# A graph layer on one core: a new order of the sums, scans, powers and table terms over the five steps of a turn

## The chip, the core and the metric

The kernel runs on one core of a Trainium2 chip. The metric is the device time of one execution in microseconds. Before the change the median of three runs is 2198.17 us (2196.62 to 2205.42). The core has five engines that run side by side, each strictly in the order of its own queue: PE (TensorE, matrix products), DVE (VectorE), ACT (ScalarE), POOL (GpSimd, here the issuer of the gathers) and SP (the issuer of nearly all other transfers).

## What is computed

The layer has 12,500 nodes of 128 features and 212,500 edges, sorted by the node they point to (dst). Cut to what matters:

```python
h  = maximum(layernorm(x), 0)
q  = h @ Wq.T + bq;  v = h @ Wv.T + bv          # per node, 8 heads of 16
k  = edge_attr @ Wk.T + bk                      # per edge
in_m   = sum(q[src] * k,      over the 16 of a head)
out_m  = sum(q[dst] * k,      over the 16 of a head)
diag_m = sum(q[src] * q[dst], over the 16 of a head)
score = (segment_softmax(in_m / 4, dst) + segment_softmax(out_m / 4, dst)
         + segment_softmax(diag_m / 4, dst)) * edge_weight ** lam
out = segment_sum(score * v[dst], dst) @ Wo.T + bo
return x + leaky_relu(out, 0.1)
```

## The kernel before

**Staging.** A first part (some 130 us) normalizes the nodes, makes q and writes it to a table in memory, turns the edge indices, and writes a second table, `q3_table`, that holds q as three bf16 terms whose sum is q. The borders of the edges' segments are made behind the table of q. Then comes the main loop of 415 steps: step g takes a block of 512 edges. Five steps s = 0 to 4 make a turn t; the five blocks of a turn come from five far-apart parts of the sorted edge list, so that five parts are scanned side by side (120 rows: 5 parts x 24 logits). There are 83 turns. A short tail closes the last turns and the last nodes.

**One step.** POOL fetches q[src] of the 512 edges by four indirect gathers (tile `qq`, line 694), started up to 20 steps ahead (`LOOK`); a gather of step g + 20 may start when PE is through with step g. PE projects the edge features to k (L1165 the bias, L1167 the products) and spreads q[dst] over the edges by a one-hot product (L1175), both into one of two buffers of `kq_ps`; it also transposes the features of the step after (L1158). PE makes the k of step g + 1 in step g, so it has to wait until DVE's products of step g - 1 have freed the buffer. ACT copies q[dst] out (`qd`, L1178), copies the transposed features (`eT`, L1160) and makes one-hots (L1152, L1153). DVE multiplies (`prod`, L1188 and L1189), and a sum over the heads makes the logits (L1194, `lT`). Two steps share one `prod` tile: the sum runs over a pair of steps, or over the one step left over, as five is odd.

**One turn.** Spread over the steps, each turn also has:

- `turn_logits`: PE transposes the turn's logits to rows (`l_ps`, L1215); `scan_on`: DVE scans them forward for the running maximum of each segment (`u`, L1248, and a short `head`, L1253). This is done for turn t - 1.
- `spread_far` (ACT, L1259), then `scan_back`: DVE scans backward (`m`, L1266); `turn_max`: PE transposes the maxima back (`m_ps`, L1336). This and the rest is for turn t - 2.
- `powers`: DVE subtracts the maxima (`back`, L1344), ACT takes the exponentials (L1345); `weigh_powers`: DVE multiplies by the edge weights (L1356).
- `show_ends`: PE makes selection matrices (`d_ps`, L1370), ACT shapes them (`sel`, L1373 twice, L1374); `to_rows`: PE sums by node (`w_ps`, L1384), ACT copies (L1389), SP adds the rows to memory (L1400).
- `other_terms`: for 40 of the turns, the three bf16 terms of the next 256 nodes' q: SP loads them, ACT rounds (L1288), DVE subtracts (L1289), ACT rounds again (L1291), DVE subtracts (L1292), SP writes (L665).
- Nodes: 20 pairs of 256 nodes each are finished within the loop, each over four turns: `scores` (L1034 to L1040), `turn` (PE L1084, ACT `hT` L1087), `project_v` (PE L1090, L1092) and `weigh` (DVE L1100) in the first two turns; `turn`, `project_o` (PE, then ACT L1111) and `add_x` (DVE L1116, L1117) in the next.

**What sets the order.** The order is written out by hand: `pin` ties every instruction behind the one recorded before it on its engine. Within a step the main loop calls, in this order, `nodes_before`, the gather, `project`, `spread_q`, `turn`, `logits`, `one_hots`, then the piece of the turn for this s, the fetches and stores of rows, `nodes_between` and (for s below 3) `other_terms`. All small PSUM results (`l_ps`, `far_ps`, `m_ps`, `d_ps`, `w_ps`, `node_ps`) share three buffers in rotation, so each one waits for the release of the third before it.

## Time and profile before

| | us |
|---|---|
| median of three runs | 2198.17 |
| the profiled execution | 2201.97 |
| its span (first to last instruction) | 2200.1 |
| DVE busy | 1961.2 (89% of the span) |
| PE busy | 1715.9 (78%) |
| POOL busy | 1595.9 (73%) |
| ACT busy | 1414.0 (64%) |
| mean granted TensorE clock | 0.795 of full |

In a row of a timeline the first number is the start in us from the span's start, the second the length in us; then engine, line, operation and tiles, and in brackets how long the engine sat idle before it and what ended the wait. In a list of waits, the three numbers are us in total, times, and the longest. In a table of stretches each engine's busy us stand with the number of its instructions, then the granted clock.

### The profile page before, as it was taken

The page shows a single profiled execution, that of the slowest core. Times are in us where ns is not written, and L with a number is a line of the kernel's source. Part 1 is how long each engine was busy: PE and PEld are TensorE (multiplying, and loading weights), DVE is VectorE, ACT ScalarE, POOL GpSimd, SP SyncE. Part 2 cuts the span into 40 slices and gives each one's busy share as a digit, 9 for nine tenths or more (in the row PEclk, how much of TensorE's full clock was granted, in tenths as well). Part 3 has the DMA queues.
Part 4 walks back from the last instruction along what each step waited for, and adds up shares of the span by engine and source line. Part 5 has one row for each costly group of instructions (what it writes and reads, how often), then busy time and mean ns, then how long its engine had stood idle before and what let it go on. Part 6 is the DMA issues. An engine that isn't in the chain of part 4 may idle for free.

```text
span 2200.1 us, 34526 instructions
## 1 busy us (share of the span) xinstructions
PE 1715.9 (78%) x10337; PEld 1370.5 (62%) x10337; DVE 1961.2 (89%) x2144; ACT 1414.0 (64%) x2639; POOL 1595.9 (73%) x1678
## 2 busy tenths in 40 slices
PE   7767787787878788887788778777777888877886
PEld 5556566565666666666666666666565666666665
DVE  7759999999898989899998999998999899888985
ACT  8846666566665666666666666666666666666681
POOL 5677777777777777777777777777777777777740
PEclk9868888888787877788877777887888777877787
DMA  9695545545554555555554655555555554555522
GB/s 266 177 260 148 179 146 175 156 149 181 152 156 148 181 161 158 154 156 184 157 153 152 192 159 147 158 177 154 157 158 185 153 154 145 155 162 152 161 85 64
DMA packets 306063, 355.66 MB, mean 162 GB/s; under 512 B 118195, under 2 KB 225661, under 8 KB 305557
## 3 DMA queue, kind: packets, MB, share of 16 engines
q1 hardware_dynamic: 237094, 238.23, 35.0%
q0 software_dynamic: 53184, 108.92, 17.6%
q10 hardware_dynamic: 15588, 6.22, 1.1%
q8 instruction: 83, 1.36, 0.2%
q14 instruction: 114, 0.93, 0.1%
HBM read 321.34 MB, written 31.85 MB: 161 GB/s over the span
## 4 chain that ended last, share of the span: by engine, by line
PE 37%; DVE 28%; DMA 12%; issue 10%; ACT 5%; POOL 3%; SPq 1%; DVEq 0%; ACTq 0%; POOLq 0%
PE kq_ps L1167 13%; DMA qq<-q_table,src_i 12%; DVE prod L1189 9%; DVE lT L1194 8%; PE w_ps L1384 6%; PE eT_ps L1158 5%; DVE prod L1188 5%; PE kq_ps L1165 3%; DVE u L1248 3%; PE kq_ps L1175 3%; POOL qq L694 3%; PE node_ps L1092 3%; PE d_ps L1370 2%; PE l_ps L1215 1%; ACT eT L1160 1%
## 5 line engine op out<-in xcount | busy, mean ns | idle before, releaser
L694 POOL DMA_INDIRECT qq<-q_table,src_i x1620 | 1544.5, 953 | 493.7 <-issue 232.5
L1167 PEld LDWEIGHTS kq_ps<-wk,eT 128*128 128x128 f32 x3320 | 524.5, 241 | 371.0 <-issue 154.4
L1194 DVE TENSOR_REDUCE lT<-prod 128x192 f32<-128x3072 f32 (+1 forms) x249 | 702.1, 2820 | 8.6
L1167 PE MATMUL kq_ps<-wk,eT 128*128 128x128 f32 x3320 | 619.8, 344 | 8.6 <-ACT eT L1160 8.2
L1178 ACT COPY qd<-kq_ps 128x512 f32<-128x512 f32 x415 | 242.3, 584 | 426.2 <-PE kq_ps L1175 396.1
L1189 DVE TENSOR_TENSOR prod<-qq,kq_ps 128x1024 f32<-128x1024 f32 x415 | 503.4, 1213 | 0.0
L1165 PE MATMUL kq_ps<-b,ones 3*128 3x512 bf16 x415 | 184.6, 445 | 217.8 <-DVE prod L1189 217.8
L1158 PE MATMUL eT_ps<-ident,ea 128*128 128x128 f32 x1660 | 324.4, 331 | 1.0 <-DVE qq L944 1.0
L1152 ACT ACTIVATE relb<-relb,before 114x512 bf16<-114x512 bf16 x415 | 302.6, 729 | 0.0
L1188 DVE TENSOR_TENSOR prod<-qd,kq_ps 128x512 f32<-128x512 f32 x415 | 279.8, 674 | 12.5 <-ACT qd L1178 7.7
L1153 ACT ACTIVATE oh<-relb 114x512 bf16<-114x512 bf16 x415 | 261.4, 630 | 13.6 <-ACT relb L1152 0.4
L1160 ACT COPY eT<-eT_ps 128x512 f32<-128x512 f32 x415 | 244.0, 588 | 36.6 <-PE eT_ps L1158 36.0
L1384 PE MATMUL w_ps<-back,sel 128*114 128x144 f32 (+1 forms) x1344 | 215.5, 322 | 20.5 <-DVE back L1356 11.7
L1158 PEld LDWEIGHTS eT_ps<-ident,ea 128*128 128x128 f32 x1660 | 229.8, 175 | 1.1 <-DVE qq L944 1.1
L1384 PEld LDWEIGHTS w_ps<-back,sel 128*114 128x114 f32 (+1 forms) x1344 | 207.8, 213 | 27.0 <-ACT sel L1374 10.1
L1336 PE MATMUL m_ps<-ident,m 120*128 120x120 f32 x332 | 69.8, 342 | 176.0 <-DVE m L1266 176.0
L1175 PE MATMUL kq_ps<-win,oh 114*128 114x128 bf16 x1660 | 199.9, 255 | 2.7 <-DMA win<-q_table 2.7
L1248 DVE TENSOR_TENSOR_SCAN u<-far,u,l_ps 120x512 f32<-120x512 bf16 x82 | 104.7, 1277 | 94.2 <-PE l_ps L1215 88.2
L1345 ACT ACTIVATE back<-back 128x480 f32<-128x480 f32 x83 | 50.1, 604 | 202.9 <-DVE back L1344 202.9
L1336 PEld LDWEIGHTS m_ps<-ident,m 120*128 120x128 f32 x332 | 49.7, 214 | 198.5 <-DVE m L1266 195.7
L1175 PEld LDWEIGHTS <-oh 114*128 114x128 bf16 x1660 | 161.2, 118 | 15.6 <-issue 2.9
L1266 DVE TENSOR_TENSOR_SCAN m<-far_ps,head,u 120x512 f32<-120x512 f32 x81 | 103.2, 1274 | 0.0
(194 smaller groups left out, 1481.2 us busy)
## 6 DMA issues: line engine op xcount, KB each, us to landing
ea<-in_edge_attr_dram SPq DMA_DIRECT2D x83, 1280.0 KB
relb<-rel_d SPq DMA_DIRECT2D x83, 640.0 KB
qq<-q_table,src_i POOLq DMA_INDIRECT x1620
win<-q_table SPq DMA_DIRECT2D x415, 28.5 KB
far<-far_d SPq DMA_DIRECT2D x84, 120.2 KB
q_table<-more_q SPq DMA_DIRECT2D x40, 192.0 KB
sums<-rows SPq DMA_DIRECT2D x408, 7.1 KB
q_table<-xq SPq DMA_DIRECT2D x24, 256.0 KB
```

The lines of the kernel that those rows point to most:

```text
L694: rows = pin(nc.gpsimd.indirect_dma_start(out=qq[:, j, :], out_offset=None, in_=x if g < RAW else q_table, in_offset=bass.IndirectOffsetOn ...
L1152: pin(nc.scalar.activation(d, d, AF.Abs, bias=before[:K3]))
L1153: pin(nc.scalar.activation(oh, d, AF.Relu, bias=1.0, scale=-1.0))
L1158: pin(nc.tensor.transpose(eT_ps[:, j, :], eas[g // S][:, g % S, j * F:(j + 1) * F], ident))
L1160: pin(nc.scalar.copy(eT, eT_ps))
L1165: pin(nc.tensor.matmul(k_ps, ones3, bk3, start=True, stop=False))
L1167: pin(nc.tensor.matmul(k_ps[:, j, :], eTs[g][:, j, :], wk, start=False, stop=(j == JN - 1)))
L1175: pin(nc.tensor.matmul(qd_ps[:, j, :], ohs[g][:, j * P:(j + 1) * P], d["win"][:, s, :], start=(j == 0), stop=(j == JN - 1)))
L1188: pin(nc.vector.tensor_mul(prod[:, :, 2, :], qds[g], kqs[g][:, 0]))
L1189: pin(nc.vector.tensor_mul(prod[:, :, 0:2, :], qqs[g][:, :, None, :].to_broadcast([P, JN, 2, F]), kqs[g].rearrange("p i j f -> p j i f")))
L1194: pin(nc.vector.tensor_reduce(lTs[t][:, :, lo:s + 1, :].rearrange("p j s c -> p j (s c)"), prods[0][:, :, :s + 1 - lo].rearrange("p j s i ...
L1384: pin(nc.tensor.matmul(w_ps[:, i].rearrange("p s c -> p (s c)"), d["sel"][:n, j, lo:lo + 3, :].rearrange("p s w -> p (s w)"), d["back"][:n ...
```

## The change

The same work is done; only its place in the turn differs.

- The pairs of the sum are cut otherwise: step 0 alone, then steps 1 and 2, then 3 and 4 (before: 0 and 1, 2 and 3, then 4 alone).
- `scan_on` moves from step 0 to step 1, right ahead of `scan_back`.
- `powers` moves from step 2 to step 3, behind `show_ends`; `weigh_powers` stays in step 3 but goes to the end of the step, behind the nodes' work and `other_terms`.
- `other_terms` is spread over steps 1, 3, 4 and the next turn's step 0, begins one turn earlier, and has two buffers for each of its tiles.
- Nodes: `project_o` moves from step 4 to step 2, `add_x` from 4 to 3, `scores` from 0 to 3.

```diff
-            if s % 2 == 0:
+            lo = max(0, s - 1 + s % 2)
+            if s == lo:
                 prods[0] = work.tile([P, JN, 2, 3, F], F32, name="prod", bufs=1)
-            prod = prods[0][:, :, s % 2]
+            prod = prods[0][:, :, s - lo]
...
-            if s % 2 == 1 or s == S - 1:
-                lo = s - s % 2
+            if s % 2 == 0:
                 pin(nc.vector.tensor_reduce(
...
         def other_terms(t, s):
 
-            if s == 0 and other_units and due_at[other_units[0]] <= t + 5:
-                held["u"] = other_units.pop(0)
-            if not held:
-                return
-            u = held["u"]
-            if s == 0:
-                held["q"] = work.tile([P, 2, F], F32, name="more_q", bufs=1)
+            if s == 0 and "u" in held:
+                q3 = held["q3"]
+                pin(nc.vector.tensor_sub(q3[:, :, 2, :], held["q"], q3[:, :, 1, :]))
+                put_terms(held["u"], q3)
+                held.clear()
+            if s == 0 and other_units and due_at[other_units[0]] <= t + 6:
+                u = held["u"] = other_units.pop(0)
+                held["q"] = work.tile([P, 2, F], F32, name="more_q", bufs=2)
                 pin(nc.sync.dma_start(held["q"].rearrange("p k f -> p (k f)"),
                                       units(q_table, u, 1, F)[:, 0, :]))
-            elif s == 2:
-                q3 = held["q3"] = work.tile([P, 2, 3, F], BF, name="more_q3", bufs=1)
-                pin(nc.scalar.copy(q3[:, :, 0, :], held["q"]))
-                pin(nc.vector.tensor_sub(held["q"], held["q"], q3[:, :, 0, :]))
+            if "u" not in held:
+                return
+            if s == 1:
+                held["q3"] = work.tile([P, 2, 3, F], BF, name="more_q3", bufs=2)
+                pin(nc.scalar.copy(held["q3"][:, :, 0, :], held["q"]))
             elif s == 3:
+                pin(nc.vector.tensor_sub(held["q"], held["q"], held["q3"][:, :, 0, :]))
+            elif s == 4:
                 pin(nc.scalar.copy(held["q3"][:, :, 1, :], held["q"]))
-                pin(nc.vector.tensor_sub(held["q3"][:, :, 2, :], held["q"], held["q3"][:, :, 1, :]))
-                put_terms(u, held["q3"])
-                held.clear()
...
-            if old and t % 2 == 0 and s == 4:
+            if old and t % 2 == 0 and s == 2:
                 old.project_o(small([P, JN, F], "node_ps"))
...
-            if new and not even and s == 0:
+            if new and not even and s == 3:
                 new.scores()
...
-            if old and even and s == 4:
+            if old and even and s == 3:
                 old.add_x(nc.vector)
...
             if s == 0:
                 if t > 0:
                     turn_logits(t - 1)
-                    scan_on(t - 1)
...
             elif s == 1:
+                later(scan_on, t - 1)
                 later(scan_back, t - 2)
...
             elif s == 2:
                 later(turn_max, t - 2)
-                later(powers, t - 2)
                 fetch_places(t + 2)
             elif s == 3:
                 later(show_ends, t - 2)
-                later(weigh_powers, t - 2)
-                other_terms(t, s)
+                later(powers, t - 2)
                 fetch(t + 2)
...
-            if s < 3:
-                other_terms(t, s)
+            other_terms(t, s)
+            if s == 3:
+                later(weigh_powers, t - 2)
```

The two product lines become 1189 and 1190, and the lines behind `other_terms` move down by one (L1344 becomes L1345). On DVE, the queue around the two scans. Before (u is the forward scan, m the backward one, lT the sums, ab and score the nodes' scores):

```order
L1188 TENSOR_TENSOR prod<-qd,kq_ps 128x4x128
L1189 TENSOR_TENSOR prod<-qq,kq_ps 128x4x256
L1248 SCALAR_TENSOR_TENSOR u<-far,u,l_ps 120x512
L1253 SCALAR_TENSOR_TENSOR head<-far,u 120x64
L1034 TENSOR_TENSOR ab<-ab 128x4x48
...
L1040 TENSOR_TENSOR score<-score,ab 128x32
L1188 TENSOR_TENSOR prod<-qd,kq_ps 128x4x128
L1189 TENSOR_TENSOR prod<-qq,kq_ps 128x4x256
L1194 TENSOR_REDUCE lT<-prod 128x4x48
L1266 SCALAR_TENSOR_TENSOR m<-far_ps,head,u 120x512
```

and with the change, from step 0 on:

```order
L1189 TENSOR_TENSOR prod<-qd,kq_ps 128x4x128
L1190 TENSOR_TENSOR prod<-qq,kq_ps 128x4x256
L1194 TENSOR_REDUCE lT<-prod 128x4x24
L1189 TENSOR_TENSOR prod<-qd,kq_ps 128x4x128
L1190 TENSOR_TENSOR prod<-qq,kq_ps 128x4x256
L1248 SCALAR_TENSOR_TENSOR u<-far,u,l_ps 120x512
L1253 SCALAR_TENSOR_TENSOR head<-far,u 120x64
L1266 SCALAR_TENSOR_TENSOR m<-far_ps,head,u 120x512
```

The forward scan now stands a whole step behind the products of step 0, and the backward one directly behind it, ahead of the pair's sum instead of behind it.

On DVE again, the powers, in a turn with a unit of `other_terms` (and, in the second, with an `add_x`). Before:

```order
L1344 TENSOR_TENSOR back<-lT,m_ps 128x20x24
L1289 TENSOR_TENSOR more_q<-more_q,more_q_11655 128x256
L1188 TENSOR_TENSOR prod<-qd,kq_ps 128x4x128
L1189 TENSOR_TENSOR prod<-qq,kq_ps 128x4x256
L1194 TENSOR_REDUCE lT<-prod 128x4x48
L1356 TENSOR_TENSOR back<-back,att_t 128x20x24
```

With the change:

```order
L1194 TENSOR_REDUCE lT<-prod 128x4x48
L1189 TENSOR_TENSOR prod<-qd,kq_ps 128x4x128
L1190 TENSOR_TENSOR prod<-qq,kq_ps 128x4x256
L1345 TENSOR_TENSOR back<-lT,m_ps 128x20x24
L1116 TENSOR_TENSOR h<-h,node_ps 128x512
L1117 TENSOR_TENSOR x_in<-h,x_in 128x512
L1293 TENSOR_TENSOR more_q<-more_q,more_q_11359 128x256
L1357 TENSOR_TENSOR back<-back,att_t 128x20x24
```

A step's products and a pair's sum stood between the subtraction and the weighing; now only nodes' work and a subtraction of `other_terms` stand there, in the turns that have them.

On ACT, the exponentials of the same step (`sel` is the selection matrix, `back` the powers). Before:

```order
L1345 ACTIVATE back<-back 128x20x24
L1288 CAST more_q_12139<-more_q 128x2x128
L1178 COPY qd<-kq_ps 128x512
L1160 COPY eT<-eT_ps 128x512
L1152 ACTIVATE relb<-relb,before 114x512
L1153 ACTIVATE oh<-relb 114x512
L1373 ACTIVATE sel<-d_ps 128x380 x2
L1374 ACTIVATE sel<-sel 128x760
```

With the change:

```order
L1178 COPY qd<-kq_ps 128x512
L1160 COPY eT<-eT_ps 128x512
L1152 ACTIVATE relb<-relb,before 114x512
L1153 ACTIVATE oh<-relb 114x512
L1374 ACTIVATE sel<-d_ps 128x380 x2
L1375 ACTIVATE sel<-sel 128x760
L1346 ACTIVATE back<-back 128x20x24
```

The exponentials stood ahead of the four regular instructions of a step and the three of `sel`; now they stand behind them.

## The prediction

> **What bounds the kernel now.** I read the page's busy times first, then how fast each engine moves through the main loop.
>
> ```profile
> PE 1715.9 (78%) x10337; PEld 1370.5 (62%) x10337; DVE 1961.2 (89%) x2144; ACT 1414.0 (64%) x2639; POOL 1595.9 (73%) x1678
> L694 POOL DMA_INDIRECT qq<-q_table,src_i x1620 | 1544.5, 953 | 493.7 <-issue 232.5
> ```
>
> DVE is the busiest, but POOL's 73% misleads: its gathers take 953 ns, and nearly each has 0.30 us of idle time ahead of it that no other engine can shorten. The next two views cut the span at 200 and 2100 us; the first counts gathers (L694), the second the first product of each step (L1188).
>
> ```profile
> 0.00:200.00 200.00, 132.13 (x132) 0.85 0.77 222
> 200.00:2100.00 1900.00, 1439.01 (x1513) 0.79 0.53 160
> 2100.00:2200.00 100.00, 15.17 (x16) 0.77 0.22 65
> ```
>
> ```profile
> 0.00:200.00 200.00, 11.52 (x17) 0.85 0.77 222
> 200.00:2100.00 1900.00, 262.55 (x390) 0.79 0.53 160
> ```
>
> POOL: 1900/1513 = 1.256 us a gather, so 25.1 us for the 20 gathers of a turn. DVE: 1900/390 = 4.87 us a step, so 24.4 us a turn. At 200 us, 132 gathers are out (33 steps) against 17 steps of products: a lead of 16. At 2100 us the lead is 411 - 407, some 4 to 5 steps. So there are two limits. DVE with its waits sets the pace now, but it runs after gathers that go at an unalterable 25.1 us a turn, and has nearly caught them. A faster DVE can gain only what is left of the lead. The third view is what DVE waits for, over the span:
>
> ```profile
> DVE u L1248 <- PE l_ps L1215: 88.2, 49, 4.1
> DVE more_q L1289 <- ACT more_q L1288: 52.4, 40, 4.6
> DVE prod L1188 <- ACT qd L1178: 7.7, 8, 3.2
> ```
>
> **What the change removes.** The forward scan u asks for PE's transposed logits one step later: DVE has the products of another step (about 1.9 us) and a sum in between, so the 88.2 us go. The first subtraction of `other_terms` comes two steps behind ACT's rounding instead of at once, so the 52.4 us go. That is 140.6/83 = 1.69 us a turn. Each instruction's work is the same; the sums are again two of a pair and one of a single step.
>
> **What it adds: the weighing right behind the powers.** This is the dearest term. Here is a turn of before from step 2 on, with PE's transposes of its logits as the last row:
>
> ```profile
> 1218.57 1.08 PE L1336 MATMUL m_ps<-ident,m 120*128 120x120 f32 x4 [2.45 <-DVE m L1266]
> 1219.01 1.22 DVE L1189 TENSOR_TENSOR prod<-qq,kq_ps 128x1024 f32<-128x1024 f32 x1
> 1220.14 0.65 DVE L1344 TENSOR_TENSOR back<-lT,m_ps 128x480 f32<-128x480 f32 x1
> 1220.79 2.08 PE L1167 MATMUL kq_ps<-wk,eT 128*128 128x128 f32 x8
> 1220.82 0.60 ACT L1345 ACTIVATE back<-back 128x480 f32<-128x480 f32 x1 [2.75 <-DVE back L1344]
> 1221.75 0.42 DVE L1289 TENSOR_TENSOR more_q<-more_q,more_q 128x256 f32<-128x256 f32 x1 [0.96 <-ACT more_q L1288]
> 1222.09 0.68 DVE L1188 TENSOR_TENSOR prod<-qd,kq_ps 128x512 f32<-128x512 f32 x1
> 1223.94 3.35 DVE L1194 TENSOR_REDUCE lT<-prod 128x192 f32<-128x3072 f32 x1
> 1224.18 0.59 ACT L1160 COPY eT<-eT_ps 128x512 f32<-128x512 f32 x1 [0.27 <-PE eT_ps L1158]
> 1224.68 0.63 PE L1165 MATMUL kq_ps<-b,ones 3*128 3x512 bf16 x1
> 1225.41 0.63 ACT L1153 ACTIVATE oh<-relb 114x512 bf16<-114x512 bf16 x1
> 1226.83 0.84 ACT L1374 ACTIVATE sel<-sel 128x760 f32<-128x760 f32 x1
> 1227.21 0.65 DVE L1356 TENSOR_TENSOR back<-back,att_t 128x480 f32<-128x480 f32 x1
> 1232.51 0.60 PE L1215 MATMUL l_ps<-ident,lT 128*120 128x128 f32 x4
> ```
>
> Call the end of step 2's products T: 1219.01 + 1.22 = 1220.23. From T on PE may make k for step 4, and ACT's chain follows PE; that is the same in both orders. ACT is through with `sel` at 1226.83 + 0.84 = T + 7.44. In the new order the exponentials (0.60) come behind it: T + 8.04. DVE, meanwhile, does the pair's sum (3.35), the products of step 3 (1222.09 to 1223.94, 1.85) and the subtraction (0.65): T + 5.85. Then comes the weighing, which waits 2.19 us. Before, ACT did the exponentials at once, and a step's products and a sum covered them. Behind the waiting DVE stand step 4's products, and PE's `w_ps` waits for the weighing.
>
> That is a turn with PE's clock low. Here is one with PE quick (1.16 instead of 2.08):
>
> ```profile
> 413.59 1.21 DVE L1189 TENSOR_TENSOR prod<-qq,kq_ps 128x1024 f32<-128x1024 f32 x1
> 415.16 1.16 PE L1167 MATMUL kq_ps<-wk,eT 128*128 128x128 f32 x8
> 420.29 0.84 ACT L1374 ACTIVATE sel<-sel 128x760 f32<-128x760 f32 x1
> ```
>
> T is 414.80, `sel` ends at T + 6.33, the exponentials at T + 6.93: a wait of 1.08. Some work of DVE fills the wait. In the 40 turns with a unit of `other_terms` its subtraction does (0.42, L1289 above): 0.42 x 40/83 = 0.2 a turn. In 20 turns the nodes' scores do:
>
> ```profile
> 1012.41 0.33 DVE L1034 TENSOR_TENSOR ab<-ab 128x192 f32<-128x192 f32 x1
> 1014.33 0.19 DVE L1040 TENSOR_TENSOR score<-score,ab 128x32 f32<-128x32 f32 x1
> ```
>
> They last 2.1 us, as long as the longer wait: worth the whole wait in 20 of 83 turns. The `add_x` of 20 other turns fills it too, but there the second `d_ps` gets its buffer only when `add_x` has read `node_ps`, which makes `sel` later by about as much; I count nothing. At the low clock: 2.19 - 0.2 - 2.19 x 0.24 = 1.5 us a turn; at the high one 1.08 - 0.2 - 0.26 = 0.6. I take the middle, 1.05: the granted clock of 0.79 in the loop says that both states are common.
>
> The Trainium skill, "TensorE: Matmul & The Clock Gate", Part 1 (the HAM clock gate), says that PE falls to half its clock after a mostly idle window of about 3.4 us and comes back after a busy one. By that rule the change would help PE, since the 2.45 us for which PE waited on m (first row of the turn above) goes, and the lower of the two prices would hold: 0.6. This trace agrees that PE is slow (2.08 against 1.16) right behind that wait. Against it, PE gets a new wait in the same place, as the pair's sum of 3.35 us now lies between the products of steps 2 and 3.
>
> **What it adds: `project_o` behind its own turn.** In 20 turns PE now makes `project_o` (0.63 + 2.08 us in the slow state, as L1165 and L1167 have in the turn above) ahead of step 3's k, right behind the transposes that ACT has yet to copy out, and behind a buffer that u must free. Cover is u, head, m and a pair's sum on DVE. Nothing from below; 2.7 us from above, 2.7 x 20/83 = 0.65 a turn; I take 0.25, since the cover is longer than the work.
>
> The other edits I put at nothing. SP's load of a unit's q comes one step ahead of the rounding instead of two; ACT is idle 36% of the time and could wait there. The stores come earlier with respect to when they are needed, three steps, and nothing on SP but fetches for two turns later stands behind them; without that cover an ACT wait would push `qd`.
>
> **The sum.** Removed 1.69, added 1.05 + 0.25 = 1.30: DVE's turn falls by 0.39 us, to 24.0. Over 81 turns that is 32 us, more than the lead allows. What the lead allows:
>
> ```profile
> 2118.80 0.94 POOL L694 DMA_INDIRECT qq<-q_table,src_i x1 [0.30 <-PE node_ps L1084]
> ```
>
> ```profile
> 2141.03 1.21 DVE L1189 TENSOR_TENSOR prod<-qq,kq_ps 128x1024 f32<-128x1024 f32 x1
> 2142.28 1.75 DVE L1194 TENSOR_REDUCE lT<-prod 128x96 f32<-128x1536 f32 x1
> 2145.27 1.27 DVE L1248 TENSOR_TENSOR_SCAN u<-far,u,l_ps 120x512 f32<-120x512 bf16 x1
> ```
>
> ```profile
> 1003.19 2.42 DMA qq<-q_table,src_i
> ```
>
> The last gather starts at 2118.80 and lands after some 2.42 us, at 2121.2; the last products then end no sooner than 2122.4. Before, they ended at 2142.24. I give DVE 1 us behind the gather: 2123.4, a gain of 18.8. The tail gives back 1.2: the last sum is now a pair's (3.35, not 1.75), PE's transposes follow it (0.60, last row of the turn above, and some 0.2 for the two hand-overs, an estimate), and the scan starts some 4.2 us behind the products instead of 3.0. So 2200.1 - 17.6 = 2182.5 of span. The median of the runs lies 1.9 below the span, so 2180.6; as the lead runs out only late (18.8/0.39 = 48 turns) and unevenly, I say 2183. The bounds of the two added terms give DVE 0.6 + 0 - 1.69 = -1.1 us a turn (capped by the gathers at the same 2181) and 1.5 + 0.65 - 1.69 = +0.46 us a turn: 2198.2 + 37 + 1.2 = 2237.
>
> **The rivals.**
>
> *The gathers set the end* (forecast): 2183, its own range 2178 to 2190. For it: DVE's two largest waits go for sure, and 18.8/81 = 0.23 us a turn is enough to arrive there. Against: it needs the new wait to stay below 1.46 us a turn.
>
> *One wait for another*: the wait for the exponentials costs about the 1.69 that was saved, and only the tail's 1.2 is left: 2199, within 11 us either way. For it: the 2.19 of the plain slow turn is close to what goes.
>
> *Slower: the weighing waits at the low clock in most turns.* The place is step 3; the price 1.5 us a turn there and up to 0.65 for `project_o`; it decides once the two pass 1.69. For it: PE's new idle stretch during the pair's sum may keep the clock low just there, and `w_ps` then starts late and pushes the next k. Against: scores and subtractions fill part of it. At +0.3 us a turn: 2198 + 24 + 1 = 2223.
>
> That POOL itself would move is not to be had: with the lead falling from 16 steps, the 20-step limit never holds it.
>
> **How the numbers follow.** Half a per cent, 11 us, is about what a measurement of this kernel tells from no change. Forecast 0.52, one wait for another 0.20, slower 0.28. The forecast lies nearly all below 2187, so faster 0.53; same 0.19; slower 0.28. The range: from 2178, just under the gathers' limit, up to 2216, which takes in the second case and the lower part of the third.
>
> **What would show it.** In the changed profile: u no longer waits for l_ps and the subtraction of `other_terms` no longer for ACT; the weighing waits for the exponentials, about 50 to 120 us in all; DVE's products wait for a gather late in the loop; POOL's last gather still starts near 2119, and the last products end within a few us of its landing. The forecast is wrong if the weighing's wait passes 140 us in all, if PE's mean clock drops below 0.79, or if POOL's gathers show gaps beyond 0.3 us.

## The result

| | before | after |
|---|---|---|
| median of 22 runs each | 2199.28 us | 2199.93 us |
| lowest to highest | 2189.63 to 2206.34 | 2195.71 to 2207.45 |
| profiled execution, its span | 2201.97, 2200.1 | 2201.88, 2200.1 |
| mean granted TensorE clock | 0.795 | 0.832 |

The ratio of after to before is 1.0005, with a 95% interval of 0.9993 to 1.0016: no change. The prediction gave this a chance of 0.19; its time, 2183, is 17 us too low.

### The profile page after: what moved, and what is told of

Read it like the earlier page. It is cut to its first block, busy times and chain, and to the rows that moved or that the text cites. A ratio compares the mean times of both kernels' runs of the same rounds, so it can differ in the third digit from the quotient of the medians.

```text
span 2200.1 us, 34605 instructions
## 1 busy us (share of the span) xinstructions
PE 1654.2 (75%) x10337; PEld 1331.5 (61%) x10337; DVE 1980.0 (90%) x2144; ACT 1418.5 (64%) x2639; POOL 1602.8 (73%) x1678
## 3 DMA queue, kind: packets, MB, share of 16 engines
q8 instruction: 83, 1.36, 0.3%
## 4 chain that ended last, share of the span: by engine, by line
DVE 29%; PE 23%; DMA 18%; issue 11%; ACT 11%; POOL 2%; ACTq 1%; SPq 1%; DVEq 1%; POOLq 0%
DMA qq<-q_table,src_i 16%; DVE prod L1190 11%; PE kq_ps L1167 9%; DVE lT L1194 8%; PE w_ps L1385 4%; DVE prod L1189 3%; PE kq_ps L1165 3%; PE eT_ps L1158 2%; POOL qq L694 2%; DVE u L1248 2%; ACT relb L1152 2%; PE kq_ps L1175 2%; ACT eT L1160 2%; ACT oh L1153 2%; PE node_ps L1092 2%
## 5 line engine op out<-in xcount | busy, mean ns | idle before, releaser
L694 POOL DMA_INDIRECT qq<-q_table,src_i x1620 | 1551.6, 958 | 494.0 <-issue 234.2
L1167 PEld LDWEIGHTS kq_ps<-wk,eT 128*128 128x128 f32 x3320 | 490.1, 227 | 446.2 <-ACT relb L1152 113.6
L1167 PE MATMUL kq_ps<-wk,eT 128*128 128x128 f32 x3320 | 582.8, 329 | 11.7 <-ACT eT L1160 11.0
L1165 PE MATMUL kq_ps<-b,ones 3*128 3x512 bf16 x415 | 176.2, 425 | 291.3 <-DVE prod L1190 290.8
L1189 DVE TENSOR_TENSOR prod<-qd,kq_ps 128x512 f32<-128x512 f32 x415 | 281.8, 679 | 41.6 <-ACT qd L1178 21.6
L1158 PE MATMUL eT_ps<-ident,ea 128*128 128x128 f32 x1660 | 316.8, 325 | 1.2 <-DVE qq L944 1.2
L1385 PE MATMUL w_ps<-back,sel 128*114 128x144 f32 (+1 forms) x1344 | 236.4, 343 | 19.4 <-DVE back L1357 19.4
L1385 PEld LDWEIGHTS w_ps<-back,sel 128*114 128x114 f32 (+1 forms) x1344 | 228.0, 230 | 27.0 <-issue 16.3
L1158 PEld LDWEIGHTS eT_ps<-ident,ea 128*128 128x128 f32 x1660 | 225.2, 172 | 1.4 <-DVE qq L944 1.4
L1357 DVE TENSOR_TENSOR back<-back,att_t 128x480 f32<-128x480 f32 x84 | 55.0, 656 | 82.3 <-ACT back L1346 82.3
L1165 PEld LDWEIGHTS <-ones 3*128 3x128 bf16 x415 | 38.9, 94 | 110.3 <-issue 99.8
L1337 PE MATMUL m_ps<-ident,m 120*128 120x120 f32 x332 | 67.3, 336 | 34.9 <-DVE m L1266 33.6
```

The lines of the kernel that those rows point to most:

```text
L694: rows = pin(nc.gpsimd.indirect_dma_start(out=qq[:, j, :], out_offset=None, in_=x if g < RAW else q_table, in_offset=bass.IndirectOffsetOn ...
L1158: pin(nc.tensor.transpose(eT_ps[:, j, :], eas[g // S][:, g % S, j * F:(j + 1) * F], ident))
L1165: pin(nc.tensor.matmul(k_ps, ones3, bk3, start=True, stop=False))
L1167: pin(nc.tensor.matmul(k_ps[:, j, :], eTs[g][:, j, :], wk, start=False, stop=(j == JN - 1)))
L1189: pin(nc.vector.tensor_mul(prod[:, :, 2, :], qds[g], kqs[g][:, 0]))
L1385: pin(nc.tensor.matmul(w_ps[:, i].rearrange("p s c -> p (s c)"), d["sel"][:n, j, lo:lo + 3, :].rearrange("p s w -> p (s w)"), d["back"][:n ...
```

## The profile after

First the busy times of the page, and its row of the gathers.

```profile
PE 1654.2 (75%) x10337; PEld 1331.5 (61%) x10337; DVE 1980.0 (90%) x2144; ACT 1418.5 (64%) x2639; POOL 1602.8 (73%) x1678
L694 POOL DMA_INDIRECT qq<-q_table,src_i x1620 | 1551.6, 958 | 494.0 <-issue 234.2
```

DVE does the same 2144 instructions and is busy 18.8 us longer than before (1961.2). A gather takes 958 ns on the average instead of 953. PE is busy 62 us less: its clock is higher.

The waits of DVE over the span (total us, times, longest):

```profile
DVE back L1357 <- ACT back L1346: 82.3, 57, 4.5
DVE prod L1190 <- DMA qq<-q_table,src_i: 22.4, 16, 3.1
DVE prod L1189 <- ACT qd L1178: 21.6, 8, 5.0
```

The 88.2 us of u for l_ps and the 52.4 us of the terms for ACT are gone. In their place stand the 82.3 us of the weighing for the exponentials, 0.99 us a turn over 83 turns, and products that wait for a gather.

Two stretches of 200 to 2100 us, by the gathers (L694) and by the first product of a step (L1189), and then the busy time of DVE in it, of before (x1666) and of after (x1663):

```profile
200.00:2100.00 1900.00, 1440.14 (x1508) 0.83 0.53 161
```

```profile
200.00:2100.00 1900.00, 265.44 (x391) 0.83 0.53 161
```

```profile
200.00:2100.00 1900.00, 1738.57 (x1666) 0.79 0.53 160
```

```profile
200.00:2100.00 1900.00, 1759.94 (x1663) 0.83 0.53 161
```

DVE starts 391 steps in these 1900 us; before, 390. Its idle time fell from 161.4 to 140.1 us, and its busy time rose by 21.4 us for the same work. So the waits went, and DVE spent as much time in another way. The page's chain of work that ended last says where the limit has moved, before and then after:

```profile
PE 37%; DVE 28%; DMA 12%; issue 10%; ACT 5%; POOL 3%; SPq 1%; DVEq 0%; ACTq 0%; POOLq 0%
```

```profile
DVE 29%; PE 23%; DMA 18%; issue 11%; ACT 11%; POOL 2%; ACTq 1%; SPq 1%; DVEq 1%; POOLq 0%
```

Before, PE has the largest share of the chain, and it is the 37% that the prediction did not read: it took DVE's waits for time that is lost on DVE alone.

**Where the busy time comes from.** A piece of DVE's timeline after (start, length):

```profile
1013.14 3.35 DVE L1194 TENSOR_REDUCE lT<-prod 128x192 f32<-128x3072 f32 x1
1016.60 0.69 DVE L1189 TENSOR_TENSOR prod<-qd,kq_ps 128x512 f32<-128x512 f32 x1
1017.20 1.21 DVE L1190 TENSOR_TENSOR prod<-qq,kq_ps 128x1024 f32<-128x1024 f32 x1
...
1034.21 0.34 DVE L1253 TENSOR_TENSOR_SCAN head<-far,u 120x64 f32<-120x64 bf16 x1
1034.65 1.28 DVE L1266 TENSOR_TENSOR_SCAN m<-far_ps,head,u 120x512 f32<-120x512 f32 x1
1035.85 0.66 DVE L1189 TENSOR_TENSOR prod<-qd,kq_ps 128x512 f32<-128x512 f32 x1
```

The sum ends at 1013.14 + 3.35 = 1016.49 and the product, which writes the tile that the sum has read, begins 0.11 us later; m begins 0.10 us after head, which it reads. The products that follow one another (1016.60 + 0.69 = 1017.29 against 1017.20) overlap by 0.09, and so do m and the product behind it (0.08). So such a pair of neighbours costs 0.19 us more than a pair that has nothing to do with each other. (A sum that reads the product in front of it, as in either kernel, begins only 0.03 us late, 162 times in the steps below.) From step 20 to step 290 (54 turns) a sum has a product right behind it 118 times after and 31 times before; head has m behind it 54 times after and never before. Worked out from all rows of DVE's timeline between these two steps:

| us | span | instructions | + waits | + other gaps | - overlap |
|---|---|---|---|---|---|
| before | 1308.9 | 1266.5 | 87.9 | 15.8 | 61.3 |
| after | 1296.0 | 1269.7 | 52.1 | 27.9 | 53.6 |

The waits fell by 35.8 us, 0.66 a turn. Gaps, lost overlap and slightly longer instructions took back 12.1 + 7.7 + 3.2 = 23.0, 0.43 a turn. What is left is 0.24 a turn.

**What became of the gain.** It had grown to 13 us at step 320 (1658.2 against 1671.5). From 1638 us on products wait for gathers. This is one of them, as the chain of waits shows its transfer, and the product itself:

```profile
1884.90 5.77 DMA qq<-q_table,src_i
```

```profile
1890.79 1.22 DVE L1190 TENSOR_TENSOR prod<-qq,kq_ps 128x1024 f32<-128x1024 f32 x1 [3.09 <-DMA qq<-q_table,src_i]
```

The gather lands 5.77 us after its start, not 2.42 as in the one that the prediction had taken. The chain of before already had slow ones: its 77 rows of gathers go from 2.27 us to the 6.06 of this one.

```profile
1009.43 6.06 DMA qq<-q_table,src_i
```

And the last gather starts later:

```profile
2126.68 0.95 POOL L694 DMA_INDIRECT qq<-q_table,src_i  x1 [0.30 <-issue]
```

That is 7.9 us behind before's 2118.80. Then comes the last turn, on DVE:

```profile
2122.17 0.69 DVE L1189 TENSOR_TENSOR prod<-qd,kq_ps 128x512 f32<-128x512 f32 x1 [0.81 <-ACT qd L1178]
...
2132.12 0.69 DVE L1189 TENSOR_TENSOR prod<-qd,kq_ps 128x512 f32<-128x512 f32 x1 [4.74 <-ACT qd L1178]
...
2140.06 0.66 DVE L1357 TENSOR_TENSOR back<-back,att_t 128x480 f32<-128x480 f32 x1 [4.23 <-ACT back L1346]
2140.63 0.68 DVE L1189 TENSOR_TENSOR prod<-qd,kq_ps 128x512 f32<-128x512 f32 x1
```

And of before the same stretch, from step 2 to step 4:

```profile
2129.27 0.69 DVE L1188 TENSOR_TENSOR prod<-qd,kq_ps 128x512 f32<-128x512 f32 x1 [0.29 <-ACT qd L1178]
...
2140.44 0.68 DVE L1188 TENSOR_TENSOR prod<-qd,kq_ps 128x512 f32<-128x512 f32 x1
```

Step 2 of the last turn begins 7.1 us sooner than before; step 4 begins 0.2 us later (18.46 us against 11.17). PE shows the reason for the 4.74 us:

```profile
2124.70 0.37 PE L1090 MATMUL node_ps<-b,ones 3*128 3x512 bf16 x1 [1.23 <-ACT sel L1374]
2126.42 2.08 PE L1092 MATMUL node_ps<-wo,hT 128*128 128x128 f32 x8 [1.35 <-ACT hT L1087]
2128.43 0.60 PE L1165 MATMUL kq_ps<-b,ones 3*128 3x512 bf16 x1
2128.96 2.08 PE L1167 MATMUL kq_ps<-wk,eT 128*128 128x128 f32 x8
```

`project_o` stands ahead of step 3's k, waits for a buffer and for `hT`, and both run at the low clock. In the last turn ACT has three further `sel` to shape and the last nodes to normalize; the exponentials start at 2139.44, 4.9 us after their subtraction on DVE has ended: that is the 4.23.

## The experiments

The kernels of one table row were run on one chip, beside the kernel before on that chip. "1 run" means a profile and one time.

| kernel | median us | before there | ratio, 95% interval |
|---|---|---|---|
| last_old | 2194.83 | 2199.55 | 0.9971, 0.9951 to 0.9992 |
| powers_in_2 | 2199.84 | 2199.55 | 0.9989, 0.9965 to 1.0013 |
| free_after | 2197.39 | 2199.55 | 0.9981, 0.9955 to 1.0006 |
| free_before | 2207.94 | 2199.55 | 1.0017, 0.9989 to 1.0045 |
| only_terms | 2204.62 | 2197.58 | 1.0032, 1.0012 to 1.0053 |
| only_sums_scan | 2188.12 | 2197.58 | 0.9965, 0.9948 to 0.9983 |
| p2_last_o4 | 2190.84 (11 runs up to 2192.53, one of 3212.69) | 2197.58 | 0.9971, 0.9953 to 0.9990 |
| slots | 2199.06 | 2204.39 | 0.9975, 0.9953 to 0.9996 |
| project_o_in_4 | 2193.87 | 2204.39 | 0.9948, 0.9925 to 0.9971 |
| sums_scan_terms | 2197.16 | 2204.39 | 0.9966, 0.9948 to 0.9984 |
| sums_scan_terms_slots | 2194.79 | 2204.39 | 0.9959, 0.9936 to 0.9982 |
| before_c, after_c, dbl_after, p2_last_o4_c | 2196.18, 2199.73, 2226.64, 2188.55 | 2194.90 | 1 run each |

### The last turn in the old order: last_old

```diff
             elif s == 2:
                 later(turn_max, t - 2)
+                if t == G - 1:
+                    powers(t - 2)
...
-                later(powers, t - 2)
+                if t < G - 1:
+                    later(powers, t - 2)
...
-            if old and t % 2 == 0 and s == 2:
+            if old and t % 2 == 0 and s == (4 if t == G - 1 else 2):
```

(and `add_x` in step 4 there.)

> The changed kernel, with the old order in the last turn alone: there the exponentials come in step 2 again, and project_o and add_x in step 4. Theory 'gathers and last turn' (the change quickens VectorE until the gathers hold it, from about 1600 us, and the last turn then loses what is left, 4.74 us before step 3 and 4.23 us before the weighing): from step 2 to step 4 the kernel before needs 2140.44 - 2129.27 = 11.2 us, the changed one 18.5; so the last step begins some 7 us sooner and the span is 2191 to 2195, ratio to before 0.996 to 0.998. Theory 'one wait for another' (the loop as a whole lost as much as it won, the last turn is no special place): the loop's pace is that of the changed kernel, and the time stays within 2 us of it, 2198 to 2202.

Measured: 2194.83 and a span of 2191.5, as the first theory had it. The rows of its last turn, steps 2 and 4:

```profile
2120.39 0.69 DVE L1189 TENSOR_TENSOR prod<-qd,kq_ps 128x512 f32<-128x512 f32 x1 [1.65 <-ACT qd L1178]
...
2129.99 0.69 DVE L1189 TENSOR_TENSOR prod<-qd,kq_ps 128x512 f32<-128x512 f32 x1 [1.53 <-ACT qd L1178]
```

9.6 us instead of 18.46, with the loop unchanged. Its last products end at 2131.81, and its last gather starts at 2124.30: with 5.8 us to land and 1.2 for the product, 2131.3 was the earliest. So the last turn cost the change what the loop had won, and without that cost the gathers set the end.

### The exponentials early in every turn: powers_in_2

```diff
             elif s == 2:
                 later(turn_max, t - 2)
+                later(powers, t - 2)
...
-                later(powers, t - 2)
```

> The changed kernel with the subtraction and the exponentials back in step 2 in every turn; the weighing stays at the end of step 3. Both theories: the wait of the weighing for the exponentials, 82.3 us in the changed kernel, falls below 10 us. 'One wait for another': what is freed shows in the time, 60 to 80 us less, about 2125. 'Gathers and last turn': VectorE is up to 1 us a turn quicker, has used up its lead by about 900 us instead of 1600, and from there on waits for the gathers, 50 to 80 us in all instead of 22.4; only the last turn's 4.2 us before the weighing are won, so 2194 to 2198.

Measured: 2199.84, a little above what the gathers' theory had, and not the 2125 of the other. The wait of the weighing fell to 3.6 us after 200 us; this came instead:

```profile
DVE prod L1190 <- DMA qq<-q_table,src_i: 99.9, 47, 4.0
```

DVE does step 140 at 750.8 us, 28 us sooner than after, and from about then on goes at the gathers' pace: step 320 begins at 1657.2, against 1658.2 after. The predicted limit exists. It makes the 82.3 us of the weighing worth nothing in a version that meets it.

### Without the gathers' limit: free_after, free_before

```diff
-            for j in of:
+            for j in [j for j in of if g < RAW or j < 3]:
...
-                                     qqs[g][:, :, None, :].to_broadcast([P, JN, 2, F]),
+                                     qqs[g][:, 0:1, None, :].to_broadcast([P, JN, 2, F]),
```

> The changed kernel with three of the four gathers of a step (from the second turn on), and the products reading the first column of q[src] for all four, so that a part of q[src] is left out and GpSimd needs 18.8 us a turn instead of 25.1. To be read against free_before. 'Gathers and last turn': without the gathers' limit the changed kernel keeps its pace of 24.0 us a turn (steps 20 to 290) to the end; its last turn begins some 15 to 20 us before that of free_before, and 6 to 11 us of it are left at the end (the last turn loses 9): 2185 to 2195 if VectorE's own instructions take as long as before. 'One wait for another': both variants end within 4 us of each other.

> The kernel before with the same gathers left out. It never waited for a gather, so both theories expect its own pace, 24.2 to 24.7 us a turn, and 2190 to 2202; lower only as far as fewer gathers leave SBUF to VectorE.

Measured: 2197.39 and 2207.94, both above the ranges expected. The intervals overlap, and the 10.6 us between the medians are not certain: the two profiled executions took 2201.5 and 2191.6 us, the other way round. In them VectorE needs 1304.8 and 1300.5 us for steps 20 to 290. So there is no large gain of the change that only the gathers hide; how large the small one is, these two leave open.

### One part alone: only_terms, only_sums_scan

`only_terms` is the kernel before with the new `other_terms`; `only_sums_scan` the kernel before with the new pairs of sums and `scan_on` in step 1.

> The kernel before with the new other_terms alone: load, rounding, first and second subtraction spread over the steps 0, 1, 3, 4 and 0. Theory 'gathers and last turn': the wait of 52.4 us goes, nothing is added and the last turn keeps its old order, so VectorE gains up to 0.6 us a turn, comes within a few steps of the gathers late in the loop, and the last step begins 8 to 14 us sooner: 2185 to 2192, ratio 0.994 to 0.997. Theory 'one wait for another': the wait for l_ps grows by what the terms no longer wait, 2196 to 2202.

> The kernel before with the new pairs of sums and the forward scan in step 1 alone. Both theories: the wait for l_ps (88.2 us) goes. 'Gathers and last turn': against it stand about 0.19 us for each sum that has a product right behind it (about 2 a turn more) and for the scan m right behind head, 0.5 us a turn or so, so VectorE gains about 0.5 us a turn; the last turn has no jam; the tail gives back 1.4: 2187 to 2195. 'One wait for another': the exponentials and the terms are still where they were, so the wait comes up at the subtraction of the terms or at the products, 2196 to 2202.

Waits of DVE in `only_terms`, and then in `only_sums_scan`:

```profile
DVE u L1248 <- PE l_ps L1215: 141.9, 67, 4.3
```

```profile
DVE more_q L1292 <- ACT more_q L1291: 60.6, 40, 4.1
DVE more_q L1289 <- ACT more_q L1288: 46.6, 40, 2.0
```

Spreading the terms alone is slower by 0.3%: the 52.4 us come up again at l_ps, 141.9 instead of 88.2 (77.4 in `before_again`, on the same chip). Moving the scan alone makes the terms wait 107.2 instead of 52.4. We read this so: while both are there, each gives PE and ACT the time that the other would otherwise wait. Towards the end, where the terms run out (the last first subtraction is at 1788 us in the kernel before), the moved scan does pay: steps 290 to 412 take 581.5 us in `only_sums_scan` and 602.9 in the kernel before. On this point "one wait for another" was right for each part alone.

### Both waits removed, the weighing left where it was: sums_scan_terms

> The kernel before with the pairs of sums, the scan in step 1 and the spread terms; powers, weighing, project_o, add_x and the scores keep their old places. Theory 'the two waits only go together' (alone, the wait for the terms came up at l_ps, 140 us instead of 88, and the wait for l_ps came up at the terms, 98 instead of 52): without both, VectorE runs 22.5 to 23.5 us a turn up to step 140, meets the gathers before step 200 and waits for them 60 to 100 us; the last step begins within 4 us of the last gather's landing: 2186 to 2192, ratio 0.994 to 0.997. Theory 'one wait for another': a third wait takes their place and the pace stays above 24 us a turn with less than 20 us of waits for gathers.

> The same with the product tile of slots. If the gathers set the end, as the first theory has it, VectorE's shorter hand-overs turn up as longer waits for gathers, 10 us more, and the time is that of sums_scan_terms within 2 us; if VectorE's pace sets it, 10 to 15 us less.

Waits of `sums_scan_terms`:

```profile
DVE prod L1190 <- DMA qq<-q_table,src_i: 88.3, 43, 4.7
DVE prod L1190 <- issue: 29.3, 14, 4.1
```

From step 20 to step 140, before the gathers hold it, DVE needs 538.5 us, of which 0.6 are waits (before: 568.3 and 32.7; after: 564.1 and 19.1). That is 1.24 us a turn less than before, where the first profile of after has 0.18. So the two removals together are worth nearly what the prediction had summed (1.36 us a turn of waits were there in this stretch), and the place of the powers and the weighing, with `project_o` and the scores, costs 1.07 of it, hand-overs included. Other profiles of the same loop, `last_old`, `after_c` and (but for the product tile) `slots`, need 569.1 to 571.2 us here, which makes it up to 1.36. `powers_in_2`, which differs from after in the place of the subtraction and the exponentials alone, needs 540.5: nearly all of the price is theirs. From about step 140 on `sums_scan_terms` stands at the gathers; its last one starts at 2127.11, and of the early gain its time, 2197.16 instead of the expected 2186 to 2192, shows little. The version with `slots` is the same within its spread.

### The hand-over: slots

```diff
-            if s == lo:
+            if g == 0:
                 prods[0] = work.tile([P, JN, 2, 3, F], F32, name="prod", bufs=1)
-            prod = prods[0][:, :, s - lo]
+            prod = prods[0][:, :, 1 if s == 0 else s - lo]
...
-                    prods[0][:, :, :s + 1 - lo].rearrange(
+                    prods[0][:, :, 1 if s == 0 else 0:2].rearrange(
```

> The changed kernel with one product tile for the whole loop, in which the single step (step 0) uses the second half, so that step 1's products need not wait for the sum of step 0 to have read it. Same instructions in the same order. In the changed kernel a product that stands right behind a sum begins 0.107 us after the sum's end, 118 times between steps 20 and 290; where VectorE's neighbours are independent they overlap by 0.08 us. Theory 'hand-overs' (the shared product tile makes these gaps): the 54 pairs between step 0 and step 1 overlap again, about 64 are left, and small gaps plus lost overlap fall by some 54 x 0.19 = 10 us over these 270 steps. Theory 'any instruction behind a sum starts late': they stay 118. The time itself: within 4 us of the changed kernel by both, as the gathers and the last turn set the end.

Two pairs of a sum and a product from its timeline, a single step's sum and a pair's:

```profile
1032.86 1.75 DVE L1194 TENSOR_REDUCE lT<-prod 128x96 f32<-128x1536 f32 x1
1034.53 0.68 DVE L1189 TENSOR_TENSOR prod<-qd,kq_ps 128x512 f32<-128x512 f32 x1
...
1040.99 3.36 DVE L1194 TENSOR_REDUCE lT<-prod 128x192 f32<-128x3072 f32 x1
1044.45 0.69 DVE L1189 TENSOR_TENSOR prod<-qd,kq_ps 128x512 f32<-128x512 f32 x1
```

Behind the single sum, whose half of the tile the product does not write, the product now overlaps by 0.08 us; behind the pair's sum, whose half it does write, it still begins 0.10 us late. Between steps 20 and 290 this holds for all 22 pairs of the first kind (0.10 us late in after) and all 96 of the second. So the shared tile makes the gap, not the sum. The expected 54 pairs were miscounted: in the other turns a terms' or a nodes' instruction stands between. So 4 us were won, not 10, and the time is after's within its spread.

### project_o back in step 4: project_o_in_4

```diff
-            if old and t % 2 == 0 and s == 2:
+            if old and t % 2 == 0 and s == 4:
                 old.project_o(small([P, JN, F], "node_ps"))
...
-            if old and even and s == 3:
+            if old and even and s == 4:
                 old.add_x(nc.vector)
```

> The changed kernel with project_o and add_x back in step 4 in every turn. It prices the term that the prediction put at 0.25 us a turn: PE's waits at node_ps for ACT's sel and hT (36.6 and 36.4 us) go. If they cost VectorE anything, its pace from step 20 to 290 (24.0 us a turn) falls by up to 0.25 us; if they lie under other work, it stays within 0.1 us, or the weighing waits longer, as add_x no longer covers it. In the last turn the jam of 4.74 us goes and the late weighing of 4.2 us stays: 2194 to 2199.

Measured: 2193.87, the lowest ratio of all. Steps 20 to 290 take 1290.9 us, 5 to 11 less than in the four kernels that differ in nothing else there or only in the slots (1296.0, 1302.2, 1302.0, 1299.9): 0.1 to 0.2 a turn, near the predicted 0.25. But up to step 140 it is no quicker (574.7 us against 564.1 to 571.2), and PE's waits at the bias product of `node_ps` hardly fell: 68.0 us for `sel`, instead of 36.6 for `sel` and 36.4 for `hT`. So this mean price stays unsure. The jam of the last turn is gone, the late weighing is still there:

```profile
2122.91 0.69 DVE L1189 TENSOR_TENSOR prod<-qd,kq_ps 128x512 f32<-128x512 f32 x1 [0.27 <-ACT qd L1178]
...
2129.16 0.66 DVE L1357 TENSOR_TENSOR back<-back,att_t 128x480 f32<-128x480 f32 x1 [3.88 <-ACT back L1346]
```

### The early exponentials with an easy last turn: p2_last_o4

This is `powers_in_2` with `project_o` and `add_x` in step 4 of the last turn.

> The changed kernel with powers in step 2 in every turn and project_o and add_x in step 4 in the last turn. 'Gathers and last turn': the loop is held by the gathers from about 900 us, the last turn has no jam and no late weighing, so the last product begins within 4 us of the last gather's landing (its start plus about 2.4): 2128 to 2131 instead of 2140.6, span 2189 to 2193, ratio 0.995 to 0.997. 'One wait for another': no better than powers_in_2, 2197 to 2202.

Measured: 2190.84; the profiled execution was quicker, 2184.7 of span. Its last step begins at 2123.83, 5.9 us after the start of the last gather (2117.98); the nearest of all, `only_sums_scan`, has 5.4. `powers_in_2`, with the jam, began its last step 10.4 us after its last gather.

### The late last gather: before_again, before_c, after_c, dbl_after, p2_last_o4_c

> The kernel before itself, once more, for its trace on this chip. Open is why the last gather of the changed kernel starts 7.9 us later (2126.68 against 2118.80), which is 1.2606 us a gather from 200 to 2050 us instead of 1.2561. If the new order of VectorE's work does it, this trace shows 1.256 and a last gather near 2119; if chip or run does it, 1.259 or more and a last gather near 2125, without any change.

`before_again` has 1.2563 us a gather and its last one at 2120.24: it shows what the order hypothesis asked for, but after may have run on another chip. So, on one chip:

> The kernel before, for its gathers on the same chip as the next three. If the chip or the run sets the pace of the gathers, it has the same time a gather (200 to 2050 us) as after_c within 0.001 us; if the order does, 0.0045 less, 1.256 against 1.2605, and its last gather starts 6 to 8 us sooner than that of after_c.

> The changed kernel, for its gathers on the same chip. Chip or run: as before_c within 0.001 us. Order: 0.0045 us a gather more than before_c. In either case its own waits should be as in the first profile: the weighing 75 to 95 us, l_ps near nothing, the last turn with the jam of 4 to 5 us ahead of step 3.

> The changed kernel with each weighing done twice (the same values written again), 83 x 0.65 = 54 us more of VectorE. If the weighing lengthens the gathers beside it, the gathers over 1.0 us long grow from some 50 to 80 to 100 and the time a gather by 0.003 us; if not, both stay as in after_c. The span grows by what VectorE's lead does not hide: 54 us less the 22 us for which it waited for gathers, or 25 to 45 us.

> The kernel of p2_last_o4 again, which had 1.2555 us a gather on its chip. Chip or run: as before_c and after_c here. Its last step begins within 6 us of its last gather's start plus 2.4.

The gathers (busy us, count) of `before_c`, `after_c` and `dbl_after`, each in its 200 to 2050 us:

```profile
200.00:2050.00 1850.00, 1400.77 (x1473) 0.80 0.55 161
```

```profile
200.00:2050.00 1850.00, 1402.12 (x1470) 0.83 0.55 161
```

```profile
200.00:2050.00 1850.00, 1404.49 (x1461) 0.84 0.54 159
```

| | before_c | after_c | dbl_after | p2_last_o4_c |
|---|---|---|---|---|
| us a gather, start to start | 1.2558 | 1.2595 | 1.2667 | 1.2561 |
| gathers longer than 1.0 us | 39 | 67 | 84 | 55 |
| of these, begun during a weighing | 23 | 42 | 64 | 22 |
| last gather starts | 2118.38 | 2123.38 | 2134.46 | 2118.49 |

On one chip, with one profile each, the new order's last gather is 5.0 us late, and weighing twice makes it 11.1 us later still. The rows of `after` show how a weighing lengthens a gather, here one that takes 1.39 us instead of 0.945:

```profile
1021.19 0.65 DVE L1357 TENSOR_TENSOR back<-back,att_t 128x480 f32<-128x480 f32 x1
```

```profile
1021.27 1.39 POOL L694 DMA_INDIRECT qq<-q_table,src_i  x1 [0.30 <-DMA qq<-q_table,src_i]
```

When the gather begins, the weighing has 0.57 us left; the gather takes 0.44 us longer. In the four traces of the table, from 200 to 2050 us, 161 gathers began with more than 0.2 us of a weighing left. 148 of them took longer by just what was left less 0.12 to 0.13 us; the other 13 had begun within 0.04 us of the weighing's start, and there the weighing was the one that took longer (0.69 to 0.73 us). None of the 1961 that began so in a sum, and none of the 1787 that began so in a product, took over 1.0 us. And each of the 245 long gathers of the table began during a weighing, a subtraction of `other_terms`, an `add_x` (L1117) or an addition or product of the scores, all of them with two operands in SBUF; the products and the first line of `add_x` (L1116) have one in PSUM. So what counts is not how many gathers meet a weighing (98 in `before_c`, 103 in `after_c`) but how many begin in one. Why more do so in the changed order is open.

This is not the whole of the 7.9 us between the first two profiles. There, 53 and 51 gathers are long, and those of after add only 3.5 us more; the short ones are 1.2511 us apart instead of 1.2490, some 3.4 us over 1600 gathers. The short ones differ like that from profile to profile, on one chip too (1.2503 in `before_c`, 1.2486 in `after_c`), and why is open.

The Trainium skill, "GPSIMD Engine Reference", 1. Specifications, says that GpSimd shares its SBUF interface with VectorE and contends with instructions of VectorE that have two inputs in SBUF. The weighing is one (`back` and `att_t`), and these counts agree.

`after_c` repeats the first profile otherwise: 101.2 us of waits for the exponentials, and 17.9 us from step 2 to step 4 of the last turn; steps 20 to 290 take 1302.0 us against 1310.2 of `before_c`, 0.15 a turn. `dbl_after` took 26.9 us more than `after_c` for 54 us more of VectorE's work.

## Why the prediction was wrong, by its own steps

The forecast had the last products end 18.8 us sooner than before; they ended 0.2 us later, at 2142.44. Three steps failed. The sum of DVE's turn left out 0.43 us of hand-overs a turn, two thirds of what the waits gave back. The end that the gathers allow was put 10.3 us too early. And the last turn was priced only as part of a mean, where it cost 7.3 us at once; this took what the other two had left.

- **What is removed** was right: l_ps and the terms' first subtraction no longer stop DVE. The two could be summed only because both go; each alone came back as the other.
- **The weighing**, 1.05 us a turn in the prediction, was right: 82.3/83 = 0.99 in the first profile, 101.2/83 = 1.22 in `after_c`, and 1.07 to 1.36, hand-overs included, by the difference to `sums_scan_terms`.
- **The sum of DVE's turn** failed. It took "each instruction's work is the same" for "the same busy time". The pair's sum with a product right behind it, and m right behind head, cost 0.43 us a turn in hand-overs, with slightly longer instructions included. Without `project_o`, the predicted fall of the waits was 1.69 - 1.05 = 0.64; measured are 0.66 and 0.59. With the hand-overs it leaves 0.24 and 0.15 instead of 0.39. The prediction asked for 0.23 to arrive at the gathers: the first profile just had it, `after_c` did not.
- **`project_o`**, 0.25 a turn, is neither confirmed nor refuted as a mean (0.1 to 0.2 in one profile, and none of it up to step 140). In 18 turns its bias product waits for ACT's `hT` (36.4 us), where the prediction had it behind a buffer of u. The upper price of 2.7 us, spread over 83 turns, was the wrong way to use it: in the last turn, behind which nothing catches up, it costs 4.74, with the late weighing 18.46 - 11.17 = 7.3 us. This is the step that turned a small gain into none, as `last_old` shows.
- **The gathers as a limit that nothing moves** was half right. Once DVE is quicker, they do set the end (`powers_in_2`, `sums_scan_terms`, `p2_last_o4`). But the limit lay too low: the last gather starts later in the changed kernel (5 us on one chip, 7.9 between the two profiles, where about half is not the order's), and a gather that is waited for lands after 5.8 us, not 2.42. With 2126.68 + 5.8 + 1.2 the products could have ended at 2133.7 at the earliest, 8.5 us before 2142.24 instead of 18.8. The prediction read one row of 2.42 us where the same chain went up to 6.06.
- **The clock.** PE's wait for m fell from 176.0 to 33.6 us and the clock rose from 0.795 to 0.832, the direction of the rule that the prediction cited; the weighing's wait did not fall to the lower price of 0.6 with it.
- **The other edits**, put at nothing, did cost DVE nothing in the loop: ACT now waits for the load of a unit's q (42.5 us in 32 turns, before none), but between 150 and 2100 us DVE waits for `qd` once, 0.46 us.
- **The tail**, 1.2 us given back, was right (u starts 6.01 us behind step 4 instead of 4.83).
- None of the three signs named as proof against the forecast appeared: 82.3 is below 140, the clock rose, POOL's gaps stayed 0.30. The list had no sign for DVE's busy time, nor for the last turn.

The rival "one wait for another", 2199, has the right time by luck, for another reason: two waits went and one came, and the loop did gain 7 us at the last turn's step 2; the last turn spent it.

Seven orders have an interval wholly below 1 against before: `project_o_in_4` (0.9948), `sums_scan_terms_slots` (0.9959), `only_sums_scan` (0.9965), `sums_scan_terms` (0.9966), `last_old` and `p2_last_o4` (0.9971) and `slots` (0.9975). Their intervals overlap, so which is best is not settled, and the changed kernel was not timed beside them: the time of `slots` is that of after (2199.06 against 2199.93), and its ratio is low because before took 2204.39 on that chip. In the first six the last step begins 5 to 9 us after the last gather's start, so little is left but the gathers themselves.

## What to carry to other kernels

Before a wait of the busiest engine is counted as a gain, look at which engine leads the chain of waits: here PE had 37% of it, and a wait removed alone came back elsewhere. When instructions of one engine are reordered, count the neighbours that share a tile, too. And price the last turn by itself: what a loop hides at a mean price is paid in full where nothing follows.

## What the runs showed of the hardware that was not expected

- Two neighbours on VectorE overlap by 0.08 us when neither needs the other; a sum that reads the product in front of it begins 0.03 us late, a product behind a sum whose tile it overwrites 0.10, m behind the head it reads 0.10. In the trace the last two have a wait instruction of their own ahead of them in the queue, the sum has none; whether that makes the 0.07 us between them was not tested.
- A gather (0.945 us on POOL) that begins while a VectorE instruction with both operands in SBUF runs takes longer by what is left of that instruction less 0.12 to 0.13 us (148 of 161 begun in a weighing, up to 1.41 us in `after_c`). One already under way when the weighing begins is not (0 of 64 over 1.0 us in `before_c`).
- In `sums_scan_terms` a product that waited for a gather began a median of 6.0 us after the start of its step's last gather (43 times, 4.4 to 7.4), worked out from the timelines of POOL and DVE.
